# A two-layer decoder on one core: the last expert blocks in a branch, heads reordered, zeros by DMA, routing steps doubled

## The chip, the cores and the metric

The kernel runs on one core of one Trainium2 chip. A core has TensorE (PE, with its weight loads as PEld), VectorE (DVE), ScalarE (ACT), GpSimd (POOL) and SyncE (SP), each with a queue of its own, and 16 DMA engines that move what the queues issue. The metric is device microseconds (us) of one execution. Times from the profile come from one profiled execution.

## The reference

`x` has 4 images of 256 tokens with 256 features, `ctx_512` 4 x 256 x 64. Six blocks add to `x`, each after a layer norm: in layer 0 a latent attention (16 heads), an attention without weights of its own over the context, and a block that works on the 32 highest-scored tokens per image; in layer 1 these three:

```python
# head attention: for each token, its 16 heads attend to its 16 heads
q, k, v = (qkv[:, :, 0], qkv[:, :, 1], qkv[:, :, 2])           # each (b, n, 16, 16)
attn = jnp.einsum('bnhd,bngd->bnhg', q, k) / jnp.sqrt(jnp.float32(c))
attn = jax.nn.softmax(attn, axis=-1)
out = jnp.einsum('bnhg,bngd->bnhd', attn, v)
...
# cross attention: causal, 16 heads, keys and values from ctx_512
kv = latent_kv @ Wkv_expand.T
...
# experts: 28, the best 6 for each of the 1024 tokens
logits = x @ gate_weight.T
scores = jax.nn.softmax(logits, axis=-1)
topk_w, topk_idx = jax.lax.top_k(scores, TOP_K)
...
h = jax.nn.silu(x @ wg) * (x @ wu)
return (y + w_tok[:, None] * (h @ wd), None)
```

The inputs are drawn from a fixed seed. 1024 tokens times 6 choices are 6144 rows for the experts.

## The kernel before, in words

All of it is one program without loops on the chip: Python loops write out every instruction, and a planner (the tile framework) orders them for each engine. It goes by the order in which the program wrote them, and lets a later one go first where its inputs are ready earlier by its own estimate. Products that go through `_InOrder` (L72; the profile has them under L89 and L92) keep their written order. The written order of two pieces of work that run beside one another is made by `_side_by_side` (L54): each piece is a generator, one `yield` is one step, and the piece with the smallest share of its given number of steps done goes next.

Each of the later stages works in two halves of 512 tokens, images 0 and 1 and then 2 and 3.

*Heads and cross attention* (L534 to L569). `_head_attention` (L1203) gives two generators, `heads_a` and a second half. Per half it normalizes four row tiles (`ln_stats` with a rsqrt on POOL, L130; `h`, L146), transposes them (`h_tp`), and then takes four groups: `project` makes `pqkv` on PE and copies it on ACT, `weigh` multiplies q with k on POOL, eight heads at a time (L1270, 128x2048 elements), and sums on DVE (L1276); `combine` weights the values on DVE (L1295, L1302). At the end `o_tp` and `apo` (L1326) project out, and L1327 adds to `x`. `_cross_attention` (L1335) gives four generators: `context_kv(0)`, `context_kv(1)` and two halves. `context_kv` clears `vz` on POOL (L1368), and projects the context: `xpk` to keys, `xpv` to values, both through the two PSUM banks of tag "tp". A half waits until its pair of keys and values is there, and runs 16 steps of `scores` (`xsc`), `turned` (`x_tp`) and `values` (`xav`). L555 puts them side by side: the rest of `heads_a` and then the first cross half against `kv[0]`, the second half of the heads, and `kv[1]`. The second cross half follows alone (L567).

*Routing.* When an image leaves cross attention (`finish`, `xpo`, L1469), its generator goes on as `_route` (L585): layer norm into `R`, logits, the best six, the place of each row in its expert's list, and then twelve indirect DMAs from POOL (L676) that write the 128-row tiles of `R` into `lists` in HBM, one per choice and tile. `advance` (L1475) moves each waiting generator by one step; `half` calls it once per step of scores (L1530), and calls it in a loop when all scores are done (L1539).

*Experts.* `_blocks` (L686) makes from the counts of rows per expert the table of blocks: a block is 128 rows of one expert's list, and there is room for NBLK = 75, the most that any routing can need. A block beyond the last full list reads a list of blank rows, whose results land in rows that nobody reads. `_experts` (L731) runs the 75 blocks: SP loads `xb` four blocks ahead with an address from a register (L757), PE transposes it (`tpx`), multiplies with the gate and up weights of the block's expert (`pgu`, L781), DVE and ACT make `eh`, PE transposes (`tph`) and multiplies with the down weights (`py`, L804), ACT scales by the routing weight (`ys`), and POOL adds the rows into one of five accumulators in HBM by an indirect DMA (L809). Blocks below LATE = 41 take three accumulators in turn, the last 34 blocks the other two; the first three are read back and added to `x` (L843, L845) while the last blocks run, the other two at the end (L851 to L857).

At the start of the kernel SP fills `lists` and the accumulators from `blank`, a tile of zeros with a row number in column 256 (L513 to L524).

Of the kernel before, what the change touches and what calls it, by code (L numbers as in the profile page):

```python
# [19 lines left out]
P = 128  # L20
# [18 lines left out]
NACC = 3  # L39
NLATE, LATE = 2, NBLK - 34  # L40

# [25 lines left out]
def _in_turn(*gens):  # L67
    for gen in gens:
        yield from gen
# [34 lines left out]
def kernel(ctx: ExitStack, tc: tile.TileContext, w: dict, out: bass.AP):  # L104
# [311 lines left out]
    for _ in range(4):  # L416
# [13 lines left out]
    ms1 = mixed.enter_context(tc.tile_pool(name="mod_s", bufs=1, side="right"))  # L430
    mk = mixed.enter_context(tc.tile_pool(name="mod_k", bufs=2, side="right"))
    env = dict(
        psum=psum, sm=sm, cst=cst, ident=ident, identb=identb, maskb=maskb, tri=tri, ones=ones,
        ones_row=ones_row, layernorm=layernorm, ln_stats=ln_stats, ln_apply=ln_apply, rsqrt=rsqrt, transposed=transposed, ctxT=ctxT, neghalf=neghalf,
# [77 lines left out]
    acc = [dram.tile([B * S + P, C], F32, name=f"acc{n}") for n in range(NACC + NLATE)]  # L512
    blank = res.tile([P, ROW], F32, name="blank")  # L513
    nc.gpsimd.memset(blank, 0.0)
# [39 lines left out]
    kv = [next(cross) for _ in range(2)]  # L554
    _side_by_side((_in_turn(heads_a, next(cross)), 60), (_in_turn(kv[0], next(heads_of), kv[1]), 64))  # L555
    heads.close()
# [17 lines left out]
    for g in range(0, E, 7):  # L574
# [3 lines left out]
        )  # L578
    expert, list_row, e_all = _blocks(nc, tc, route)
    ps_stack.close()  # L580
    routing.close()
    _experts(nc, tc, x, out, dict(env, wgu=wgu, wdn=wdn, lists=lists, acc=acc, expert=expert, list_row=list_row, e_all=e_all))


# [101 lines left out]
def _blocks(nc, tc, env):  # L686
# [23 lines left out]
    nc.tensor.matmul(pe[:, 0], ones[:E], past, start=True, stop=True)  # L710
    nc.tensor.matmul(pe[:, 1], nbw, past, start=True, stop=True)
    e_all = rt1.tile([P, NBLK], F32, name="e_all")
    nc.vector.tensor_scalar(e_all, pe[:, 0], float(E - 1), None, ALU.min)
# [13 lines left out]
    nc.vector.tensor_scalar(list_row, row, float(TRASH // P), float(P), ALU.min, ALU.mult)  # L727
    return expert, list_row, e_all


def _experts(nc, tc, x, out, env):  # L731
# [4 lines left out]
    with tc.tile_pool(name="ek", bufs=2) as ek, tc.tile_pool(name="eb", bufs=AHEAD + 3) as eb, tc.tile_pool(  # L736
# [16 lines left out]
        def load(j):  # L753
            if j % ROWS == 0:
                at["row"] = values(list_row, mybir.EngineType.SP, TRASH, j, ROWS)
            xb = eb.tile([P, ROW], F32, tag="xb", name="xb")
            nc.sync.dma_start(xb, lists[bass.ds(at["row"][j % ROWS], P), :])  # L757
            return xb
# [31 lines left out]
        def down(j, hT, e, xb):  # L790
# [12 lines left out]
            for k in range(2):  # L803
# [5 lines left out]
            nc.gpsimd.indirect_dma_start(  # L809
                out=acc[j % NACC] if j < LATE else acc[NACC + (j - LATE) % NLATE],  # L810
                out_offset=bass.IndirectOffsetOnAxis(ap=xb[:, C : C + 1].bitcast(I32), axis=0),
# [13 lines left out]

        words = values(expert, mybir.EngineType.PE, (1 << 20) - 1, 0, NW)
        xbs = {j: load(j) for j in range(AHEAD)}
        xTs = {j: turned(xbs[j], 0, P, "x") for j in range(2)}
        before = None
        for j in range(NBLK):  # L830
            if j + AHEAD < NBLK:
                xbs[j + AHEAD] = load(j + AHEAD)
            h, e = gate_up(j, xTs.pop(j))
            if before is not None:
                down(*before)
            if j + 2 < NBLK:
                xTs[j + 2] = turned(xbs[j + 2], 0, P, "x")
            before = (j, turned(h, 0, MH, "h"), e, xbs.pop(j))
# [7 lines left out]
        down(*before)  # L846

# [355 lines left out]
def _head_attention(nc, tc, x, w, env):  # L1203
# [20 lines left out]
    def half(g):  # L1224
# [36 lines left out]
        def weigh(j):  # L1261
# [5 lines left out]
            for c in range(2):  # L1267
                hh = slice(8 * c, 8 * c + 8)
                pr = a2.tile([P, 8, H, D], F32, tag="qk", name="qk")
                nc.gpsimd.tensor_tensor(  # L1270
                    pr,
                    q3[:, hh].unsqueeze(2).to_broadcast([P, 8, H, D]),
                    k3.unsqueeze(1).to_broadcast([P, 8, H, D]),
                    ALU.mult,
                )
                nc.vector.tensor_reduce(s[:, hh], pr, AX.X, ALU.add)  # L1276
                yield
# [57 lines left out]
def _cross_attention(nc, tc, x, w, env):  # L1335
# [28 lines left out]
    def context_kv(bp):  # L1364
        tok = slice(bp * 512, (bp + 1) * 512)
        kz = c1.tile([P, 2, 2, 512], F32, name=f"kz{bp}")
        vz = vzs[bp]
        nc.gpsimd.memset(vz, 0.0)  # L1368
        for n in range(4):
# [150 lines left out]
    def half(bp):  # L1520
# [3 lines left out]
        for b in (2 * bp, 2 * bp + 1):  # L1524
            ss = c2.tile([P, 2, H], F32, tag="xss2", name="xss2")
            for n in range(8):
                g, e, sp = n // 4, n // 2 % 2, n % 2
                now = (f, b, g, e, sp, scores(f, b, g, e, sp, ss), ss)
                yield
                advance()  # L1530
                waiting.append(now)
                if len(waiting) > 2:
                    after(*waiting.pop(0))
                yield
        if bp == 1:
# [124 lines left out]
```

## Time and profile before

| | |
|---|---|
| time, median of 3 runs | 972.06 us (971.18 to 975.4) |
| the profiled execution | 971.14 us |
| its span, first to last instruction | 969.3 us |
| PE busy | 772.9 us, 80% |
| DVE busy | 546.7 us, 56% |
| POOL busy | 332.8 us, 34% |
| ACT busy | 306.5 us, 32% |
| mean granted clock of TensorE | 0.838 |

| stretch of the span | what runs |
|---|---|
| 0 to 440 us | layer 0, and from 305 us on the first half of the heads beside it |
| 440 to 620 | heads, first cross half, context keys and values |
| 620 to 706 | second cross half, routing of images 0 and 1 |
| 706 to 745 | routing of images 2 and 3, writes of the lists |
| 745 to 951 | 75 expert blocks |
| 951 to 969 | last sums, output |

A line of the profile names a source line (L781), an engine, and the tiles written and read (`pgu<-wgu_e,Tx`). The chain of work is followed back from the last instruction: at each step to what released it. Busy time of PE includes matmuls that wait in its pipeline; idle time of an engine costs something only where others wait for that engine.

### The profile page before, as it was taken

The numbers are of one execution on the slowest core, as the hardware profiler recorded it, in microseconds if no ns is written. First come the engines' busy times: TensorE is split into PE (matmuls) and PEld (weight loads), VectorE is DVE, ScalarE is ACT, GpSimd is POOL, SyncE is SP. The second block draws the span as 40 slices with busy tenths as digits, with TensorE's granted clock in tenths as the row PEclk, the third lists the DMA queues.
The fourth block names the chain that finished last, engine by engine and source line by source line (L and its number), as shares of the span: only waits on it lengthen the run. The fifth ranks groups of instructions, "written<-read, shape, count | busy, mean of one in ns | idle before, by whom it ended". The sixth has DMA issues, their size and how long they took to land.

```text
span 969.3 us, 12208 instructions
## 1 busy us (share of the span) xinstructions
PE 772.9 (80%) x3740; PEld 484.5 (50%) x3740; DVE 546.7 (56%) x1334; ACT 306.5 (32%) x997; POOL 332.8 (34%) x247
## 2 busy tenths in 40 slices
PE   5989999699898675637858699977940999988992
PEld 2555556355565332414524456555530777766771
DVE  3277556966543688894499685346630333344333
ACT  1145434441521211211202343345400344433440
POOL 2022122214210357212650300053154466655663
PEclk9899989789997697675766659788875999999997
DMA  9689999101315004101000001921067466686666
GB/s 304 190 269 325 325 326 349 57 1 52 122 45 217 3 0 173 44 0 30 1 0 1 1 0 65 353 74 44 31 183 214 68 113 113 110 193 123 112 105 155
DMA packets 85902, 118.49 MB, mean 122 GB/s; under 512 B 5485, under 2 KB 73903, under 8 KB 85328
## 3 DMA queue, kind: packets, MB, share of 16 engines
q1 hardware_dynamic: 71072, 99.22, 31.5%
q0 software_dynamic: 13104, 16.92, 11.1%
q10 hardware_dynamic: 1664, 1.57, 0.5%
q8 instruction: 33, 0.54, 0.2%
q14 instruction: 29, 0.24, 0.1%
HBM read 60.66 MB, written 57.03 MB: 121 GB/s over the span
## 4 chain that ended last, share of the span: by engine, by line
PE 49%; DVE 18%; SPq 10%; POOL 7%; DMA 7%; issue 4%; ACT 4%; another core or an unknown queue 0%; DVEq 0%; ACTq 0%; POOLq 0%
PE pgu L781 9%; SPq L519 8%; PE py L804 6%; POOL qk L1270 4%; PE xsc L89 4%; PE x_tp L92 3%; DMA part<-acc 2%; DVE s L1276 2%; SPq L522 2%; PE tph L763 2%; DVE pv L1295 2%; PE tpx L763 2%; POOL lists L676 1%; DVE O L1302 1%; PE pqkv L1254 1%
## 5 line engine op out<-in xcount | busy, mean ns | idle before, releaser
L809 POOL DMA_INDIRECT acc<-ys,xb x75 | 117.1, 1562 | 95.4 <-ACT Tx L766 75.5
L781 PE MATMUL pgu<-wgu_e,Tx 128*128 x300 | 106.4, 477 | 2.1 <-issue 2.1
L330 POOL TENSOR_TENSOR pr<-pr,rs 128x512 f32<-128x512 f32 x32 | 42.0, 1311 | 166.9 <-DVE rs L328 78.2
L1270 POOL TENSOR_TENSOR qk<-qkv 128x2048 f32<-128x2048 f32 x16 | 72.0, 4523 | 71.4 <-ACT qkv L1258 42.3
L804 PE MATMUL py<-wdn_e,Th 88*128 x300 | 78.0, 382 | 0.6 <-DVE Th L768 0.6
L320 ACT ACTIVATE pr<-sc,nb 128x256 f32<-128x256 f32 x128 | 59.0, 474 | 61.4 <-DVE nb L315 61.2
L676 POOL DMA_INDIRECT lists<-R,rows x48 | 46.7, 973 | 77.6 <-DVE rows L660 46.9
L804 PEld LDWEIGHTS py<-wdn_e,Th 88*128 88x128 f32 x300 | 57.1, 191 | 21.6 <-DVE Th L768 1.0
L1413 ACT ACTIVATE xpr<-xsc,cnm 128x256 f32<-128x256 f32 (+1 forms) x128 | 52.2, 422 | 40.2 <-DVE cnm L1408 28.6
L787 DVE TENSOR_TENSOR eh<-pgu,sg 128x176 f32<-128x176 f32 x75 | 25.6, 341 | 68.8 <-ACT sg L785 37.3
L781 PEld LDWEIGHTS pgu<-wgu_e,Tx 128*128 128x128 f32 x300 | 51.8, 192 | 21.1 <-issue 4.4
L1276 DVE TENSOR_REDUCE s<-qk 128x128 f32<-128x2048 f32 x16 | 36.5, 2279 | 35.0 <-POOL qk L1270 35.0
L793 DVE SCALAR_TENSOR_TENSOR wjunk<-cst,e_all,xb 128x28 f32<-128x28 f32 x75 | 18.5, 247 | 63.7 <-ACT ys L808 44.4
L808 ACT ACTIVATE ys<-py,wsel 128x256 f32<-128x256 f32 x75 | 35.6, 474 | 43.7 <-PE py L804 41.5
L89 PE MATMUL av<-pT,ckt 128*64 128x256 f32 x256 | 41.7, 423 | 9.4 <-DVE pT L346 9.2
L311 DVE TENSOR_REDUCE nm<-sc 128x4 f32<-128x1024 f32 x32 | 39.0, 1218 | 17.5 <-PE sc L89 17.4
L785 ACT ACTIVATE sg<-pgu 128x176 f32<-128x176 f32 x75 | 23.8, 318 | 78.8 <-PE pgu L781 74.2
L89 PE MATMUL xsc<-kz,xqT 32*128 32x256 f32 (+1 forms) x256 | 41.9, 424 | 7.2 <-ACT xpr L1413 4.6
L92 PE MATMUL x_tp<-cst,xpr 128*128 128x128 f32 x192 | 37.0, 336 | 12.0 <-DVE xpT L1429 5.8
L763 PE MATMUL tpx<-cst,xb 128*128 128x128 f32 x150 | 29.3, 279 | 20.3 <-DMA xb<-lists 20.3
L89 PE MATMUL sc<-ckv,qk 64*128 64x256 f32 x256 | 41.0, 422 | 1.5 <-ACT qk L298 0.7
L92 PE MATMUL tp<-cst,pr 128*128 128x128 f32 x256 | 38.0, 289 | 3.3 <-DVE pT L346 2.4
(318 smaller groups left out, 1577.9 us busy)
## 6 DMA issues: line engine op xcount, KB each, us to landing
lists<-blank SPq DMA_DIRECT2D x9, 3600.0 KB
xb<-lists SPq DMA_DIRECT2D x75, 144.0 KB
wgu_e<-in_e_gu_dram SPq DMA_DIRECT2D x4, 2464.0 KB
acc<-blank SPq DMA_DIRECT2D x5, 1152.0 KB
wdn_e<-in_e_dn_dram SPq DMA_DIRECT2D x4, 1232.0 KB
wq<-in_m_wq_dram SPq DMA_DIRECT2D x4, 1024.0 KB
mwo<-in_m_wo_dram SPq DMA_DIRECT2D x2, 2048.0 KB
part<-acc SPq DMA_DIRECT2D x16, 256.0 KB
```

The source lines that it names most:

```text
L89: self._next(self.engine.matmul(*args, **kw))
L92: self._next(self.engine.transpose(*args, **kw))
L320: nc.scalar.activation(pr[:, e, qt, :], sc[:, e, qt, :], AF.Exp, bias=nb[:, e, qt : qt + 1], accum_out=ss[:, e, qt : qt + 1],)
L519: nc.sync.dma_start(part, blank.unsqueeze(1).to_broadcast([P, 25, ROW]))
L676: put = nc.gpsimd.indirect_dma_start(out=lists, out_offset=bass.IndirectOffsetOnAxis(ap=rows[:, i, n : n + 1], axis=0), in_=R[:, i, :], in ...
L763: nc.tensor.transpose(tp[:m, k, :], src[:, c0 + k * m : c0 + (k + 1) * m], ident)
L781: nc.tensor.matmul(pg, xT[:, k, :], wgu[:, bass.ds(e * (4 * M) + k * 2 * M, 2 * M)], start=(k == 0), stop=(k == 1))
L804: nc.tensor.matmul(py, hT[:, k, :], wdn[:, bass.ds(e * (2 * C) + k * C, C)], start=(k == 0), stop=(k == 1))
L809: nc.gpsimd.indirect_dma_start(out=acc[j % NACC] if j < LATE else acc[NACC + (j - LATE) % NLATE], out_offset=bass.IndirectOffsetOnAxis(ap= ...
L1270: nc.gpsimd.tensor_tensor(pr, q3[:, hh].unsqueeze(2).to_broadcast([P, 8, H, D]), k3.unsqueeze(1).to_broadcast([P, 8, H, D]), ALU.mult,)
L1276: nc.vector.tensor_reduce(s[:, hh], pr, AX.X, ALU.add)
L1413: nc.scalar.activation(pr[:, j, cols], sc[:, j, cols], AF.Exp, bias=nm[:, i, j : j + 1], accum_out=ss[:, i, h : h + 1])
```

## The change

Five things change.

1. Blocks 64 to 74 stand in a branch (`tc.If`), ahead of blocks 0 to 63 in the program. `total`, the number of blocks that the routing needs, is one more product in `_blocks`; all engines load it and jump over the branch where it is at most 64. The loop body is the same, moved into `blocks(first, end, also)`. LATE becomes 30, so that the last 34 of the 64 blocks use the two late accumulators; blocks in the branch use the first three. The address registers are loaded for up to five blocks at a time, as before, from the start of each part.
2. The second half of the heads writes its first eight steps (norm, transposes, the first group's projection and first product), then come both pairs of context keys and values, then the rest of the heads. The numbers of the two sides are 60 and 60 instead of 60 and 64.
3. The products of q and k on POOL come as two instructions of four heads instead of one of eight. DVE's sum over them stays one instruction.
4. `vz` is cleared by two DMAs per pair from `blank` on SP's queue instead of a memset on POOL. `blank` is allocated earlier for that.
5. While the last image's scores run, `advance` is called twice per step.

```diff
-NLATE, LATE = 2, NBLK - 34
+USUAL = 64
+NLATE, LATE = 2, USUAL - 34
...
-    _side_by_side((_in_turn(heads_a, next(cross)), 60), (_in_turn(kv[0], next(heads_of), kv[1]), 64))
+    heads_b = next(heads_of)
+
+    def second():
+        for _ in range(8):
+            next(heads_b)
+            yield
+        yield from _in_turn(*kv, heads_b)
+
+    _side_by_side((_in_turn(heads_a, next(cross)), 60), (second(), 60))
...
+    pt = psum.tile([P, 8], F32, tag="tp", name="ptotal")
+    nc.tensor.matmul(pt[:1, 0:1], nb, ones[:E, 0:1], start=True, stop=True)
+    total = rt1.tile([1, 1], I32, name="total")
+    nc.vector.tensor_copy(total, pt[:1, 0:1])
...
-                out=acc[j % NACC] if j < LATE else acc[NACC + (j - LATE) % NLATE],
+                out=acc[j % NACC] if j < LATE or j >= USUAL else acc[NACC + (j - LATE) % NLATE],
...
         words = values(expert, mybir.EngineType.PE, (1 << 20) - 1, 0, NW)
-        xbs = {j: load(j) for j in range(AHEAD)}
-        xTs = {j: turned(xbs[j], 0, P, "x") for j in range(2)}
-        before = None
-        for j in range(NBLK):
...
+        xbs = {}
+
+        def blocks(first, end, also=None):
+            for j in range(first, first + AHEAD):
+                if j not in xbs:
+                    xbs[j] = load(j)
+            xTs = {j: turned(xbs[j], 0, P, "x") for j in range(first, first + 2)}
+            before = None
+            for j in range(first, end):
+                if j + AHEAD < end:
+                    xbs[j + AHEAD] = load(j + AHEAD)
+                h, e = gate_up(j, xTs.pop(j))
+                if before is not None:
+                    down(*before)
+                if j + 2 < end:
+                    xTs[j + 2] = turned(xbs[j + 2], 0, P, "x")
+                before = (j, turned(h, 0, MH, "h"), e, xbs.pop(j))
+                if also is not None:
+                    also(j)
+            down(*before)
...
+        more = nc.values_load(
+            env["total"], min_val=0, max_val=NBLK, skip_runtime_bounds_check_because="a sum of rounded counts, at most NBLK"
+        )
+        with tc.If(more > USUAL):
+            blocks(USUAL, NBLK)
+        blocks(0, USUAL, join_sums)
...
-                nc.gpsimd.tensor_tensor(
-                    pr,
-                    q3[:, hh].unsqueeze(2).to_broadcast([P, 8, H, D]),
-                    k3.unsqueeze(1).to_broadcast([P, 8, H, D]),
-                    ALU.mult,
-                )
+                for i in range(2):
+                    h0 = 8 * c + 4 * i
+                    nc.gpsimd.tensor_tensor(
+                        pr[:, 4 * i : 4 * i + 4],
+                        q3[:, h0 : h0 + 4].unsqueeze(2).to_broadcast([P, 4, H, D]),
+                        k3.unsqueeze(1).to_broadcast([P, 4, H, D]),
+                        ALU.mult,
+                    )
                 nc.vector.tensor_reduce(s[:, hh], pr, AX.X, ALU.add)
...
-        nc.gpsimd.memset(vz, 0.0)
+        for e in range(2):
+            nc.sync.dma_start(vz[:, :, e], env["blank"][:, :C].unsqueeze(1).to_broadcast([P, 4, C]))
...
                 if len(waiting) > 2:
                     after(*waiting.pop(0))
+                if b == B - 1:
+                    advance()
                 yield
```

More of the change, by code (lines that the diff above doesn't have):

```diff
@@ L431 @@
     mk = mixed.enter_context(tc.tile_pool(name="mod_k", bufs=2, side="right"))
+    blank = res.tile([P, ROW], F32, name="blank")
     env = dict(
-        psum=psum, sm=sm, cst=cst, ident=ident, identb=identb, maskb=maskb, tri=tri, ones=ones,
+        blank=blank, psum=psum, sm=sm, cst=cst, ident=ident, identb=identb, maskb=maskb, tri=tri, ones=ones,
         ones_row=ones_row, layernorm=layernorm, ln_stats=ln_stats, ln_apply=ln_apply, rsqrt=rsqrt, transposed=transposed, ctxT=ctxT, neghalf=neghalf,
@@ L512 @@
     acc = [dram.tile([B * S + P, C], F32, name=f"acc{n}") for n in range(NACC + NLATE)]
-    blank = res.tile([P, ROW], F32, name="blank")
     nc.gpsimd.memset(blank, 0.0)
@@ L578 @@
         )
-    expert, list_row, e_all = _blocks(nc, tc, route)
+    expert, list_row, e_all, total = _blocks(nc, tc, route)
     ps_stack.close()
     routing.close()
-    _experts(nc, tc, x, out, dict(env, wgu=wgu, wdn=wdn, lists=lists, acc=acc, expert=expert, list_row=list_row, e_all=e_all))
+    _experts(nc, tc, x, out, dict(env, wgu=wgu, wdn=wdn, lists=lists, acc=acc, expert=expert, list_row=list_row, e_all=e_all, total=total))
 def _route(nc, tc, x, b, env):
@@ L727, in _blocks @@
     nc.vector.tensor_scalar(list_row, row, float(TRASH // P), float(P), ALU.min, ALU.mult)
-    return expert, list_row, e_all
+    return expert, list_row, e_all, total
 def _experts(nc, tc, x, out, env):
@@ L753, in load @@
         def load(j):
-            if j % ROWS == 0:
-                at["row"] = values(list_row, mybir.EngineType.SP, TRASH, j, ROWS)
+            if j not in at:
+                n = min(ROWS, (USUAL if j < USUAL else NBLK) - j)
+                for i, r in enumerate(values(list_row, mybir.EngineType.SP, TRASH, j, n)):
+                    at[j + i] = r
             xb = eb.tile([P, ROW], F32, tag="xb", name="xb")
-            nc.sync.dma_start(xb, lists[bass.ds(at["row"][j % ROWS], P), :])
+            nc.sync.dma_start(xb, lists[bass.ds(at.pop(j), P), :])
             return xb
@@ L826, in _experts, with join_sums @@
         words = values(expert, mybir.EngineType.PE, (1 << 20) - 1, 0, NW)
-        xbs = {j: load(j) for j in range(AHEAD)}
-        xTs = {j: turned(xbs[j], 0, P, "x") for j in range(2)}
-        before = None
-        for j in range(NBLK):
[L831 to L838, printed above, removed]
+        xbs = {}
[17 more added lines that the diff above has]
+            down(*before)
+        def join_sums(j):
             if 0 <= j - LATE - 3 < len(adds):
@@ L845, in _experts @@
                 nc.vector.tensor_tensor(x[t], x[t], parts[n, t // 2][:, t % 2, :], ALU.add)
-        down(*before)
+        more = nc.values_load(
[4 more added lines that the diff above has]
+        blocks(0, USUAL, join_sums)
         oview = out.rearrange("b (t p) c -> (b t) p c", p=P)
```

## The prediction

> **What bounds the kernel now.** I read the table of stretches first: it shows where TensorE is full and where it waits.
>
> ```profile
> 440.00:460.00 20.00, 17.65 (x35) 9.94 (x36) 8.24 (x20) 3.86 (x10) 5.48 (x6) 0.50 0.13 36
> 480.00:500.00 20.00, 16.70 (x34) 8.53 (x32) 17.68 (x26) 1.70 (x4) 9.53 (x4) 0.64 0.00 0
> 500.00:520.00 20.00, 9.36 (x34) 4.68 (x34) 18.54 (x13) 0.94 (x2) 8.23 (x2) 0.66 0.00 0
> 705.00:747.00 42.00, 8.29 (x36) 6.59 (x34) 9.50 (x54) 0.54 (x2) 23.98 (x25) 0.59 0.69 209
> 765.00:855.00 90.00, 90.00 (x429) 68.23 (x427) 33.15 (x142) 37.21 (x106) 55.96 (x36) 1.00 0.68 112
> ```
>
> Columns: the stretch, its length, then busy us of PE, PE's weight loads, DVE, ACT and POOL, granted clock, DMA share, GB/s. Three places matter. From 765 on, the expert blocks keep PE busy 90.00 us of 90 at clock 1.00: PE sets the pace. From 705 to 747 PE has 8.29 us of work: this is the tail of the routing. From 440 to 520 DVE, POOL and PE take turns.
>
> The chain of work, from the blocks' stage, shows the pace of one block:
>
> ```profile
> 764.56 1.26 PE pgu L781 x4
> 765.82 0.86 PE py L804 x4
> 767.12 1.25 PE pgu L781 x4
> ...
> 850.38 1.31 PE pgu L781 x4
> ```
>
> From 764.56 to 850.38 there are 34 blocks: 85.82 / 34 = 2.524 us each, all PE.
>
> POOL's timeline shows the tail (start, us, line, idle time before and its releaser):
>
> ```profile
> 706.64 1.05 POOL L676 DMA_INDIRECT lists<-R,rows  x1 [16.81 <-DVE rows L660]
> 714.32 0.96 POOL L676 DMA_INDIRECT lists<-R,rows  x1 [0.30 <-issue]
> 715.31 0.74 POOL L130 TENSOR_TENSOR ln_rs<-ln_ve,neghalf 128x2 f32<-128x2 f32 x1
> 726.15 0.96 POOL L676 DMA_INDIRECT lists<-R,rows  x1 [3.81 <-issue]
> 740.08 0.96 POOL L676 DMA_INDIRECT lists<-R,rows  x1 [0.30 <-issue]
> ```
>
> Image 2's twelve list writes start at 706.64, 1.27 us apart. Image 3's rsqrt, whose input was ready at 709.3 (ln_ve, DVE), stands behind seven of them until 715.31. Image 3's writes then run 726.15 to 741.04 and land at 744.9; only then does SP load the first block.
>
> The timelines of POOL and DVE at the start of the cross attention:
>
> ```profile
> 444.95 1.80 POOL L1368 MEMSET vz<- 128x2048 f32 x1
> 467.79 17.99 POOL L1270 TENSOR_TENSOR qk<-qkv 128x2048 f32<-128x2048 f32 x4 [17.84 <-ACT qkv L1258]
> 447.47 2.95 DVE L146 TENSOR_SCALAR h<-x_in,ln_mv,aln_rs 128x256 f32<-128x256 f32 x4 [0.70 <-POOL aln_rs L130]
> 472.31 2.29 DVE L1276 TENSOR_REDUCE s<-qk 128x128 f32<-128x2048 f32 x1 [21.89 <-POOL qk L1270]
> 499.02 9.68 DVE L146 TENSOR_SCALAR h<-x_in,ln_mv,cln_rs 128x256 f32<-128x256 f32 x4 [0.90 <-POOL cln_rs L130]
> ```
>
> The second half of the heads has its normalized rows at 450.4, but its first product starts at 467.79, because the context keys and values (xpk, xpv) hold PE and the two "tp" banks from 448.12 to 458.7. DVE idles 21.89 us for it.
>
> **The change part by part.** The sum is against the profiled execution, 971.14 us (span 969.3 and 1.8 around it); the median of the runs is 972.06, 0.9 above.
>
> *Blocks in a branch.* How many blocks carry tokens follows from the data: the reference's routing of its inputs gives the 28 experts 117 to 302 tokens, and their counts rounded up to 128 make 62 blocks. 62 is under 64, so blocks 64 to 74 are skipped: 11 x 2.524 = 27.8 us off, bounds 27.4 to 28.5 (single periods of 2.49 to 2.59). LATE moves from 41 to 30, so the sums of the first three accumulators stay as far from the end as now, and the stall around them (block 44 came 5.83 us after block 43, block 48 5.21 after 47) stays too. What is added: one product and one copy for `total` (the like of cnt, 0.14 us on DVE at 724.5), a load of it on all five engines, a compare and a jump. They are covered: the tables are ready at 728.4 and DVE then waits 19.03 us, PE 20.33 us, for the first block. Without that cover, if an engine can't pass the branch before the lists have landed, the row from landing to first product prices it: 744.91 to 750.79, 5.9 us. Bounds 0 to +6; I take +2, nearer to the covered end. A jump also has to find its code. The profile has the instruction queue:
>
> ```profile
> q8 instruction: 33, 0.54, 0.2%
> ```
>
> 33 packets with 0.2% of 16 engines' span: 0.002 x 16 x 969.3 / 33 = 0.94 us each, once on the jump, inside the cover. [...]
>
> The experts' words are now loaded on PE ahead of the branch. Before, the chain has 1.33 us of "issue" at 749.46 between block 0's turned rows and its first product, which I read as that load: -1.3 (0 to -2).
>
> *Routing steps doubled while the last image runs.* Image 2's route now advances twice per step of image 3. By the code its list rows came with the first advance behind image 3's eight steps, and come now with the sixth step: three steps sooner. A step's scores start 4.5 us apart here (eight of them from 662.9 to 694.1), so rows come near 705.7 - 13.5 = 692, and the twelve writes take 12 x 1.27 = 15.2, to some 708. Image 3's rsqrt finds POOL free at 709.3 instead of 715.31: -6.0. Its writes then end at 735 and the landing moves alike. The same work enters PE's queue earlier, between image 3's scores, and may hold them: 0.5 us back. -5.5; bounds -9 (if POOL's 3.81 idle goes as well) to +4 (the 3.10 us that DVE waits for PE's xpo before 685.30, once more and a little). On SP the wdn loads move with the end of cross attention.
>
> *Heads ahead of keys and values, zeros by DMA.* The two memsets leave POOL; with them go ln_ve's stretch (1.19 instead of 0.16 us) and one of h's (1.83 instead of 0.41), 2.4 us between 445.6 and 450.4. The heads' transposes no longer wait for xpv at 458.7. From them to the first product took 467.79 - 458.63 = 9.2; from 448 to 450.4 that gives 457.2 to 459.6, 8 to 10.6 sooner: -9. Keys and values of the second pair move from 606.52 to 619 on the chain (pieces of 3.30, 2.00, 1.06) into the holes of 455 to 520, where PE is busy 9.36 of 20 us: -6. Against it, the second half of the heads (38 of its 46 steps) now follows both, and thread weights 60:60 place its last x sums nearer to the last scores of the first pair. Before, 29 us lay between them (600.24) and the second pair's first scores (629.1), covered by three steps of scores; with less cover, +2. The zeros are four DMAs of 512 KB on SP, behind wxo at 446.16, with nothing behind them on SP until 600.15. The same kind of write, 3600 KB from `blank`, took about 11 us, so 1.6 each by size, and wxk's landing took 3.02: they are there before the copies into vz. Sum -13. Bounds -25 (PE idles 20.5 us between 440 and 520, and 4.5 of the stretched rows below) to +8 (xpk and xpv, 7.16 + 3.41, put in front of cross attention's own start at 510 with only 2 to 3 us hidden).
>
> *Products by four heads.* A 128x2048 product takes 4487 ns, a 128x512 one at L1032 1270 ns: 2.09 ns per element and 0.2 fixed, so two halves cost 0.2 more, 16 x 0.2 = 3.2 on POOL. About half of POOL's 72 us stands on the chain (3.8% of 969.3 = 37): +1.6. DVE instructions that run into a product stretch to its end: outside the rows of cross attention these are six between 346 and 480, longer than their kind by 0.8 to 2.2 us each, 8.2 in all; halved, -4, of which about half on the path, -2; and L1035 at 385.35, which waits for two whole products (chain: 376.51 to 385.35), may slip between: -1. In all -1.5, bounds +4 (all extra fixed costs on the path) to -8.
> The rows of cross attention themselves hold two stretched h (9.68 us for four). [...]
>
> Sum: 971.1 - 27.8 + 2 - 1.3 - 5.5 - 13 - 1.5 = 924.0; as a median 925.
>
> **Rivals.**
> *The order gives nothing.* The heads' late end uncovers the second pair's start. For it: DVE is busy 16 to 18.5 of 20 us from 480 to 580, so an earlier start may only meet it earlier. Against: its 21.89 idle. Time: 925 + 13 = 938, to 944 if the routing's gain goes too.
> *The order gives more.* Cross attention's first pair starts with the heads (516 could become 495): 925 - 12 = 913.
> *The branch is taken,* the change not doing what it says. It would need 65 blocks. No 27.8, and a second fill (5.9) and drain (946.86 to 949.1 without a next block, and some): 925 + 27.8 + 9 = 962.
> *Slower: the clock.* The blocks run at granted 1.00, the heads at 0.50 to 0.71. If the denser work ahead made the throttle grant the blocks 0.66, as from 500 to 520, 64 x 2.524 = 161.5 us become 244.7: 925 + 83 = 1008. It decides from a clock of 0.76 down: 47 us of gain and 4.9 more are 52, and 161.5 / (161.5 + 52) = 0.76. Against: every full stretch of blocks shows 1.00, and the low values stand where PE pauses.
>
> **How the numbers follow.** Forecast (914 to 937) 0.58; order gives nothing 0.22; more 0.11; branch taken 0.03; clock 0.03; the rest, mishaps that eat the gain, 0.03. The range leaves out the lower half of "more", and the last three: 906 to 945. A measurement of this kernel tells 0.5%, 4.9 us, from no change: faster 0.95, same 0.02, slower 0.03.
>
> **What would show it.** 64 groups of four pgu at 2.52 us; no xb load beyond 64; the first list write of image 2 before 700 and image 3's rsqrt with no write between its input and it; landing to first product under 5.9 us; the first product of the heads' second half some 9 us after their rows; xpk of the second pair before 520. Wrong it would be with 75 blocks, a gap of over 6 us at the branch, or a hole of PE over 15 us between heads and second pair.

## The result, and the profile after

The changed kernel takes 935.83 us (median of 933.57, 934.35, 937.30 and 953.64) beside 972.47 for the kernel before in the same session: ratio 0.9611, 95% interval 0.9574 to 0.9648. The profiled execution took 933.57 us, span 931.3 us. The forecast was 925, between 906 and 945. Some runs of these programs are about 20 us longer at a lower granted clock (below, seven of the ten of x2_old_order, the traced one among them); the ratios leave those out, which is why a ratio below can lie under that of the medians.

The span became 38.0 us shorter. The table follows both traces from stage to stage (us; the starts and ends are rows of the timelines, rounded to 0.1 us before they are subtracted).

| stage | before | after | measured | predicted |
|---|---|---|---|---|
| start to first scores of cross attention's second half | 629.1 | 618.8 | -10.3 | -14.5 |
| those to the last x sum | 78.7 | 76.8 | -1.9 | +0.5 |
| last x sum to end of the last list write | 33.2 | 27.1 | -6.1 | -6.0 |
| last list write to first expert product | 9.8 | 15.2 | +5.4 | +0.7 |
| first to last block's product | 196.0 | 169.2 | -26.8 | -27.8 |
| last block's product to the end | 22.5 | 24.2 | +1.7 | 0 |

The table of stretches of the changed kernel (columns as before):

```profile
440.00:460.00 20.00, 18.71 (x48) 9.91 (x48) 5.30 (x19) 5.17 (x15) 5.61 (x6) 0.68 0.46 142
480.00:500.00 20.00, 19.32 (x43) 11.26 (x42) 6.23 (x14) 2.74 (x7) 3.84 (x3) 0.57 0.00 0
500.00:520.00 20.00, 14.75 (x48) 7.96 (x47) 16.38 (x20) 5.36 (x25) 6.35 (x3) 0.60 0.00 1
695.00:735.00 40.00, 6.50 (x31) 5.37 (x30) 8.74 (x50) 0.25 (x1) 12.96 (x14) 0.55 0.66 182
```

From 480 to 500 the roles have changed: PE has 19.32 us of 20 (16.70 before) and POOL 3.84 (9.53). From 695 to 735, the routing's tail, PE has 6.50 us in 40: this hole has not gone, and it holds the 5.4 us that came back.

The chain of work in the blocks:

```profile
785.46 1.23 PE pgu L797 x4
...
808.13 1.29 PE pgu L797 x4
```

Nine blocks lie between: 22.67 / 9 = 2.52 us each, as before. There are 64 of them.

POOL's timeline in the tail, then the start of the heads' second half on POOL and DVE:

```profile
666.20 0.72 POOL L131 TENSOR_TENSOR ln_rs<-ln_ve,neghalf 128x2 f32<-128x2 f32 x1
680.66 1.05 POOL L685 DMA_INDIRECT lists<-R,rows  x1 [13.74 <-DVE rows L669]
694.67 0.96 POOL L685 DMA_INDIRECT lists<-R,rows  x1 [0.30 <-issue]
697.13 0.72 POOL L131 TENSOR_TENSOR ln_rs<-ln_ve,neghalf 128x2 f32<-128x2 f32 x1 [1.51 <-DVE ln_ve L142]
707.77 1.04 POOL L685 DMA_INDIRECT lists<-R,rows  x1 [9.92 <-issue]
721.78 0.96 POOL L685 DMA_INDIRECT lists<-R,rows  x1 [0.30 <-issue]
```

```profile
456.30 9.23 POOL L1304 TENSOR_TENSOR qk<-qkv 128x1024 f32<-128x1024 f32 x4 [8.69 <-ACT qkv L1290]
460.96 2.29 DVE L1310 TENSOR_REDUCE s<-qk 128x128 f32<-128x2048 f32 x1 [12.58 <-POOL qk L1304]
490.99 1.38 DVE L147 TENSOR_SCALAR h<-x_in,ln_mv,cln_rs 128x256 f32<-128x256 f32 x4 [1.12 <-POOL cln_rs L131]
```

Image 2's list writes end at 695.63, and image 3's rsqrt at 697.13 waits for its own input (DVE ln_ve) and for no write. The heads' first product is at 456.30 (467.79 before). The four h before cross attention take 1.38 us; before they took 9.68, beside POOL's products.

What came back is on SP. Its waits from 695 to 740 (us in total, times, longest), and the timelines of SP and ACT:

```profile
SPq L876 <- SPq L876: 23.2, 2, 23.0
```

```profile
733.17 5.42 SPq L773 DMA_DIRECT2D xb<-lists  x7
```

```profile
736.19 1.28 ACT L782 ACT_TABLE_LOAD   x1 [32.93 <-PE tpx L779]
737.49 0.65 ACT L782 COPY Tx<-tpx 128x256 f32<-128x256 f32 x2
740.70 1.28 ACT L801 ACT_TABLE_LOAD   x1 [2.56 <-issue]
```

SP reaches the branch (L876) at 708.18, and its next work is at 731.97. The lists land at 727.9 (DVE's wait for them ends there), but the first load leaves SP at 733.17, 5.2 us later; before, it left 0.2 us after. ACT loads its table again ahead of the first turned row (+1.28, on the path) and again for the first block's gate.

SP's own rows of the trace (start, operation, ns), above of the changed kernel and below of x8_pool_loads, where the branch's loads go by another queue:

```
708.18 COMPARE_BRANCH 50
708.38 EVENT_SEMAPHORE 17
731.40 EVENT_SEMAPHORE 17
...
731.97 TENSOR_LOAD 552

732.68 COMPARE_BRANCH 50
734.12 TENSOR_LOAD 567
```

Past the branch SP goes through eight semaphores of its own DMAs. The first of them (100 in the trace) holds it until 731.40. It is the one that the last of the four wdn loads counts up (issued on SP's queue from 695.21 on, this one at 699.08): the last packet of these loads is done at 730.9, and the last count comes at 731.39. Of the prediction's signs of being right one is missing here: from the landing of the lists to the first product it is 10.0 us (727.9 to 737.91), not under 5.9; a gap of over 6 us at the branch is what the prediction named as a sign of being wrong.

### The profile page after: what moved, and what is told of

The parts are those of the page before. It is cut to its first block, busy times and chain, and to the rows that moved or that the text cites. A ratio compares the mean times of both kernels' runs of the same rounds, so it can differ in the third digit from the quotient of the medians.

```text
span 931.3 us, 11708 instructions
## 1 busy us (share of the span) xinstructions
PE 737.9 (79%) x3610; PEld 461.0 (49%) x3610; DVE 522.0 (56%) x1291; ACT 296.4 (32%) x965; POOL 311.6 (33%) x250
## 5 line engine op out<-in xcount | busy, mean ns | idle before, releaser
L825 POOL DMA_INDIRECT acc<-ys,xb x64 | 99.7, 1558 | 91.4 <-ACT Tx L782 56.9
L1304 POOL TENSOR_TENSOR qk<-qkv 128x1024 f32<-128x1024 f32 x32 | 74.2, 2349 | 72.3 <-ACT qkv L1290 72.3
L797 PE MATMUL pgu<-wgu_e,Tx 128*128 x256 | 91.7, 481 | 0.8 <-ACT Tx L782 0.8
L820 PE MATMUL py<-wdn_e,Th 88*128 x256 | 67.0, 383 | 0.6 <-DVE Th L784 0.6
L1310 DVE TENSOR_REDUCE s<-qk 128x128 f32<-128x2048 f32 x16 | 36.6, 2285 | 41.8 <-POOL qk L1304 41.8
L820 PEld LDWEIGHTS py<-wdn_e,Th 88*128 88x128 f32 x256 | 48.7, 191 | 18.8 <-DVE Th L784 1.4
L803 DVE TENSOR_TENSOR eh<-pgu,sg 128x176 f32<-128x176 f32 x64 | 21.8, 341 | 58.4 <-ACT sg L801 58.4
L797 PEld LDWEIGHTS pgu<-wgu_e,Tx 128*128 128x128 f32 x256 | 44.5, 194 | 17.0 <-issue 1.3
L779 PE MATMUL tpx<-cst,xb 128*128 128x128 f32 x128 | 25.4, 282 | 27.1 <-DMA xb<-lists 27.1
L824 ACT ACTIVATE ys<-py,wsel 128x256 f32<-128x256 f32 x64 | 30.4, 474 | 38.0 <-PE py L820 37.4
L801 ACT ACTIVATE sg<-pgu 128x176 f32<-128x176 f32 x64 | 20.3, 318 | 65.0 <-PE pgu L797 63.9
```

The lines of the kernel that those rows point to most:

```text
L779: nc.tensor.transpose(tp[:m, k, :], src[:, c0 + k * m : c0 + (k + 1) * m], ident)
L797: nc.tensor.matmul(pg, xT[:, k, :], wgu[:, bass.ds(e * (4 * M) + k * 2 * M, 2 * M)], start=(k == 0), stop=(k == 1))
L820: nc.tensor.matmul(py, hT[:, k, :], wdn[:, bass.ds(e * (2 * C) + k * C, C)], start=(k == 0), stop=(k == 1))
L825: nc.gpsimd.indirect_dma_start(out=acc[j % NACC] if j < LATE or j >= USUAL else acc[NACC + (j - LATE) % NLATE], out_offset=bass.IndirectOf ...
L1304: nc.gpsimd.tensor_tensor(pr[:, 4 * i : 4 * i + 4], q3[:, h0 : h0 + 4].unsqueeze(2).to_broadcast([P, 4, H, D]), k3.unsqueeze(1).to_broadca ...
```

## The experiments

All times are device us; each group shared one chip. "Write to load" and "to product" are from the end of the last list write to the first xb load and the first expert product, read from each trace (the times are rounded to 0.1 us before they are subtracted).

| kernel | median | ratio, 95% interval | second half to last sum | sum to last write | write to load | to product |
|---|---|---|---|---|---|---|
| before (first trace) | 972.06 | | 78.7 | 33.2 | 4.1 | 9.8 |
| after (first trace) | 935.83 | 0.9611, 0.9574 to 0.9648 | 76.8 | 27.1 | 10.5 | 15.2 |
| x1_no_branch | 951.91 | 0.9787, 0.9709 to 0.9866 | 100.4 | 27.1 | 5.5 | 12.6 |
| x7_ahead | 960.14 | 0.9852, 0.9745 to 0.9958 | 102.7 | 27.3 | 5.6 | 12.1 |
| x8_pool_loads | 956.47 | 0.9831, 0.9750 to 0.9912 | 101.6 | 27.1 | 6.8 | 11.6 |
| x6_taken | 990.05 | 1.0168, 1.0085 to 1.0250 | 102.7 | 27.3 | 5.5 | 10.3 |
| x2_old_order | 969.83 | 0.9814, 0.9782 to 0.9846 | 88.9 | 27.3 | 10.8 | 15.6 |
| x3_eight | 933.57 | 0.9629, 0.9572 to 0.9685 | 76.6 | 27.1 | 10.4 | 15.1 |
| x4_memset | 936.00 | 0.9622, 0.9584 to 0.9660 | 75.4 | 27.3 | 10.7 | 15.5 |
| x5_single | 928.60 | 0.9556, 0.9520 to 0.9592 | 68.6 | 33.2 | 5.5 | 10.2 |
| x14_after_again | 960.97 | 0.9837, 0.9798 to 0.9877 | 99.8 | 26.8 | 10.5 | 15.1 |
| x11_wide_wdn | 955.09 | 0.9787, 0.9746 to 0.9828 | 102.8 | 27.4 | 5.0 | 9.7 |
| x12_single_wide_ahead | 942.95 | 0.9652, 0.9612 to 0.9693 | 83.9 | 33.3 | 1.7 | 11.9 |
| x10_branch_alone | 951.60 | 0.9762, 0.9706 to 0.9818 | 81.3 | 33.2 | 6.4 | 11.1 |

### First group: what the branch costs (kernel before here: 979.74)

*x1_no_branch*: no branch; blocks 64 to 74 are left out altogether.

```
-        more = nc.values_load(env["total"], ...)
-        with tc.If(more > USUAL):
-            blocks(USUAL, NBLK)
         blocks(0, USUAL, join_sums)
```

> Blocks 64 to 74 and the branch are left out of the program; `total` is still computed and nobody reads it. For these inputs the 64 blocks are enough. Theory (the branch costs 5 to 6 us between the landing of the lists and the steady blocks): landing to first product 5.9 us again or 1 to 2 less, time 5 to 7 us under the changed kernel, 929 to 931. Rival (the branch costs nothing, the lists only land later beside the wdn loads): landing to first product stays near 10 us, time within 2 us of 935.8.

*x7_ahead*: the loads of blocks 0 to 3 ahead of the branch, into buffers of their own.

```
-        xbs = {}
+        xbs = {j: load(j, "xb0", AHEAD) for j in range(AHEAD)}
```

> The loads of blocks 0 to 3 stand ahead of the branch, in four buffers of their own; all else as in the changed kernel. Theory (SP, behind the branch, waits for DMAs issued earlier, the wdn loads, before it issues the first loads): first load within 1 us of the landing, first product 3.5 to 5 us sooner, time 931 to 932. ACT still loads its table again behind the branch. Rival (the jump itself, PE's 7.1 us in the branch instruction, is what the blocks wait for): PE still gets to its first product 10 us behind the landing, time 935 to 936.

*x8_pool_loads*: inside the branch the loads go by POOL's queue.

```
+            queue, engine = (nc.sync, SP) if j < USUAL else (nc.gpsimd, Pool)
-            nc.sync.dma_start(xb, ...)
+            queue.dma_start(xb, ...)
```

> Only inside the branch, which is skipped, the loads go by POOL's queue instead of SP's. Theory (a skipped branch makes the engine whose DMAs it holds settle their counts, for which that engine waits for its earlier DMAs): SP passes at once, first load within 1.5 us of the landing, time 931 to 933; POOL settles its counts when the lists have landed, and has 18 us until its first scatter. Rival (SP waits for something other than the counts of its own DMAs): the first load stays 5.2 us behind the landing, time 935 to 936.

*x6_taken*: `more > 0`, so that all 75 blocks are computed.

> The condition is made true always, so all 75 blocks run, 64 to 74 first. Prediction's price: 27.8 for the blocks and 9 for a second fill and drain, 935.8 + 36.8 = 972.6. Rival by what the skipped branch showed (the count settling and ACT's table load come at the end of the branch either way): 4 to 6 us more, 977 to 979.

The total times of this group miss what was expected of the three that skip the blocks, and not for the branch: 24 to 26 us more than in the first trace of after lie in the second half of cross attention, which none of the edits touches. (PE and POOL run the same instructions in the same order there as in after.) The third group takes this up. The stage behind the lists can be read all the same. Without the branch the first load comes 5.5 us after the last write, and with it 10.5; 5.6 if SP has issued the first loads before the branch, and 6.8 if the branch has no loads of SP's. In x7_ahead the first product comes 3.1 us sooner than in after (12.1 against 15.2), where 3.5 to 5 were expected. Among SP's waits x8_pool_loads has none at the branch (L877); the lists are waited for:

```profile
SPq L774 <- DMA lists<-R,rows: 6.1, 1, 6.1
```

So it is not the branch as such that held SP. In after, where the skipped branch holds loads of SP's queue, SP waits 23.0 us there, until the last wdn load's count; in x8_pool_loads, where it holds none, SP does not wait there. Without the branch the first product still comes 12.6 us after the last write, because the experts' words are then loaded on PE in the path again (2.03 us) instead of ahead of it; against x8_pool_loads (11.6) the branch costs nothing there.

The chain of x6_taken, where the eleven blocks run before block 0:

```profile
781.01 1.19 PE pgu L797 x4
...
790.95 3.69 DMA acc<-ys,xb
794.83 2.14 DMA xb<-lists
797.77 2.46 PE pgu L797 x4
```

The second fill and drain put 11.75 us between the last of these blocks' products and block 0's, 9.2 more than a period. From first product to end it takes 231.9 us, x8_pool_loads 195.8: 36.1 more, where the prediction's rival had 27.8 + 9 = 36.8. ACT loads its table again here too, behind the eleven blocks (790.87, 1.28 us) and off this chain.

### Second group: the parts of the order and the routing (kernel before: 971.91)

*x2_old_order*: heads, and context keys and values, in the old order.

```
-    _side_by_side((_in_turn(heads_a, next(cross)), 60), (second(), 60))
+    _side_by_side((_in_turn(heads_a, next(cross)), 60), (_in_turn(kv[0], next(heads_of), kv[1]), 64))
```

> Only the written order of heads and context keys and values is put back (weights 60 and 64, keys and values of the first pair first); the other four parts stay. Theory (the order brings 10 to 12 us at the first cross half's start, of which some is lost again where the heads end late): first scores of the first half near 516 instead of 505, time 943 to 948. Rival (the order gives nothing, the gain there came from the zeros and the products): time within 3 us of 935.8.

*x3_eight*: one product for eight heads, as before.

```
-                for i in range(2):
...
+                nc.gpsimd.tensor_tensor(pr, q3[:, hh]..., k3..., ALU.mult)
```

> Only the products of the heads go back to eight heads at a time. Prediction's term: 1.5 us dearer, 937.3. Rival (halves only add their fixed cost, 16 x 0.2 us, and DVE's instructions pass one per half, so nothing is won): 1 to 3 us cheaper, 933 to 935.

*x4_memset*: zeros by POOL.

```
-        for e in range(2):
-            nc.sync.dma_start(vz[:, :, e], ...)
+        nc.gpsimd.memset(vz, 0.0)
```

> Only the zeros go back to memsets on POOL. Prediction's term: 2.4 us dearer, 938.2. Rival (the memsets now stand behind the first group's products and hide, since keys and values come later): within 1 us of 935.8.

*x5_single*: one routing step per step of the last image.

```
-                if b == B - 1:
-                    advance()
```

> Only the second call of advance for the last image is taken out. Prediction's term 5.5 us, the traces 6.0 from the last sum into x to the last list write: 941 to 942, with image 3's rsqrt again behind list writes of image 2. Rival (the lists wait for the wdn loads on the DMA engines, so an earlier issue does not land earlier): within 2 us of 935.8.

The order carries the gain of this part. The changed kernel itself did not run on this chip, so x3_eight stands in for it: x2_old_order against x3_eight, 0.9814 - 0.9629 = 1.85%, 18 us. By the ends of the two intervals it is between 1.0 and 2.7%, 9 to 27 us. Products by four and zeros by DMA are worth nothing that can be seen: 0.9629 and 0.9622 beside 0.9611, each well inside the others' intervals. These reach 4 to 6 us to either side, so the 1.5 and 2.4 us that were predicted could not have shown in them. DVE's rows tell the first apart, h in x3_eight and then in x2_old_order:

```profile
492.22 1.38 DVE L147 TENSOR_SCALAR h<-x_in,ln_mv,cln_rs 128x256 f32<-128x256 f32 x4 [1.12 <-POOL cln_rs L131]
```

```profile
496.89 7.41 DVE L147 TENSOR_SCALAR h<-x_in,ln_mv,cln_rs 128x256 f32<-128x256 f32 x4 [0.90 <-POOL cln_rs L131]
```

With the old order and products by four these four take 7.41 us (9.68 by eight): halving gives 2.3. With the new order no product lies beside them and they take 1.38, by eight too. The order had taken away what the halves were to mend.

Undoing the doubled routing steps makes the kernel faster, the best of all that ran: 928.6 against 933.6 and 936.0 on the same chip, 5 to 7 us. The doubling does what it says behind the last sum (33.2 to 27.1), and costs more ahead of it: the last sum comes at 695.6 in after and at 687.9 in x5_single. Together the last write ends 1.6 us later with the doubling (722.7 against 721.1). Part of the 7.7 is one hole on PE, shown here for after and then x5_single:

```profile
667.52 0.66 PE L613 MATMUL g_tp<-cst,R 128*128 128x128 f32 x2 [8.45 <-DVE R L147]
```

```profile
666.88 0.66 PE L613 MATMUL g_tp<-cst,R 128*128 128x128 f32 x2 [4.83 <-DVE R L147]
```

Both wait for image 2's rsqrt, which stands behind image 1's list writes on POOL (666.20 above). In after PE's hole is 3.6 us longer. The other 4 us I put down to the work itself, now done between the last image's steps, where the granted clock is 0.53 (from 660 to 680; 0.66 in x5_single); no run takes them apart.

The rest of the loss is the branch. In x5_single SP's settling took as long as the lists, and its first load followed at once:

```profile
SPq L876 <- SPq L876: 17.9, 2, 17.7
```

```profile
726.60 5.42 SPq L773 DMA_DIRECT2D xb<-lists  x7
```

The settling ended at 724.68, the lists' last packet at 724.5, wdn's at 724.1. The wdn loads start when cross attention ends and take 36.1, 35.4 and 36.2 us from the last sum in before, after and x5_single, whatever the routing does. In before they ended at 743.9 and the lists landed at 744.9: two bounds of the same height. The doubling lowered one of them. The traces of after and x5_single differ by 4.1 us in all: 1.6 at the last write and 5.0 from there to the first product, less 2.5 that x5_single loses again from the first product to the end (195.9 against 193.4). This loss lies between blocks 32 and 40 (28.0 us against 24.9), where the first sums are read back; x7_ahead and x8_pool_loads are as long there (27.4 and 26.4), and no run tells why.

### Third group: the wdn loads, and the chip (kernel before: 977.15)

While wdn loads, 11 packets of SP's queue are under way at a time (11.1 on average from 697 to 714 in after), and 16 while wgu loads (16.5 from 609.5 to 618). Each wdn load ends there in 11 counts of its semaphore (the last one's from 729.61 to 731.39), an xb load in 16 (734.99 to 735.32). wdn has 88 partitions.

*x14_after_again*: the changed kernel, unaltered.

> The changed kernel once more, unaltered, as the base of the three others on their chip: 933 to 938, its first xb load 10.5 us after the last list write, as in its first trace. If the long second half of cross attention that the four kernels of the first group showed (100 to 103 us from its first scores to the last x sum, instead of 77) belongs to the chip and not to those kernels, this one may show it too and be near 955.

*x11_wide_wdn*: each wdn load cut in two.

```
-        nc.sync.dma_start(wdn[:, ...], w["e_dn"][g : g + 7]...)
+        for p0, p1 in ((0, 80), (80, MH)):
+            nc.sync.dma_start(wdn[p0:p1, ...], w["e_dn"][g : g + 7, p0:p1]...)
```

> Changed kernel, each wdn load cut into partitions 0 to 79 and 80 to 87. In the trace of after, 11 packets of SP's queue are under way at a time while wdn loads (16 while the wgu loads go), and they go on to 731.0, 35.4 us after the last x sum. Theory (at the branch SP first lets its own unfinished loads land, the wdn loads among them): with 5 and 1 of 88 partitions on an engine instead of 8 they end some 35.4 x 6/8 = 26.6 us after the last sum, near 722, ahead of the lists; the first xb load then comes 4 to 6 us after the last list write instead of 10.5, and the time falls by 4 to 6 us against after on this chip. Rival 1 (the branch itself takes 5 us of SP, whatever is under way): first load still 10 to 11 us after the last write, time as after. Rival 2 (the wdn loads are held by the list writes on the same engines, not by the 11): SP's queue ends as late as before, no change.

*x12_single_wide_ahead*: x5_single's edit, this one, and x7_ahead's with the turned rows of blocks 0 and 1 ahead of the branch as well.

> Changed kernel with three edits: the last image's single routing steps, the wdn loads cut in two, and the loads of blocks 0 to 3 with the turned rows of blocks 0 and 1 ahead of the branch. Theory: x5's first product came 10.2 us after the last list write, of which 1.28 is ACT's table load behind the branch and the rest the lists' landing, the load and the turning; with the rows turned ahead of the branch the table load leaves the path, 8 to 9.5 us: 924 to 928 where x5 had 928.6, 8 to 12 below after on this chip. Rival (the wait for wdn moves from the branch to the first down product, or PE pays its 7 us branch between the turned rows and the first product): 929 to 936.

*x10_branch_alone*: the kernel before with the branch and nothing else of the change.

> The kernel before, with only the branch edited in (blocks 64 to 74, the total, the words ahead of the branch, LATE). Theory: there the wdn loads leave SP's queue near 744 and the lists land at 744.9, so that settling them costs SP little: first xb load 4 to 6 us after the last list write, 64 blocks at 2.52, ACT's table load (+1.3) against the words (-1.3): 26 to 28.5 us under before. Rival (the branch costs 5 us wherever it stands): 20 to 24 us under before.

The stretch from the last sum to the first load, in x14_after_again and then x11_wide_wdn:

```profile
718.00:756.00 38.00, 6.51 (x33) 5.32 (x31) 8.74 (x50) 0.25 (x1) 12.32 (x13) 0.56 0.67 181
```

```profile
718.00:748.00 30.00, 6.81 (x32) 5.56 (x30) 8.74 (x50) 0.25 (x1) 12.35 (x13) 0.54 0.95 227
```

The DMA share goes from 0.67 (11 / 16 = 0.69) to 0.95. The wdn loads end 29.3 us after the last sum instead of 35.1 (26.6 expected), ahead of the lists; the first load comes 5.0 us after the last write instead of 10.5, and the first product 9.7 instead of 15.1. The median falls by 5.9 us. Rival 1, a fixed price of the branch, and rival 2, wdn held by the list writes, are both out. The two ratios' intervals overlap slightly (0.9798 to 0.9877 against 0.9746 to 0.9828); the verdict on this stage rests on the traces' 5.4 us. From the first product to the end the trace of x11_wide_wdn is 2.2 us longer again (195.1 against 192.9), so how much of the 5.4 the time keeps is less sure.

x10_branch_alone does not decide by its time. Its median is 25.6 us under before, just outside what was expected (26 to 28.5); its ratio, 0.9762, is 23.3 us, inside the rival's 20 to 24, and its interval (18 to 29 us) holds both. The trace does decide: the wdn loads end at 759.1 and the lists at 758.9, SP is held by the last wdn load's semaphore until 759.53, and the first load follows at 761.00, 2.1 us behind the lists, where before it followed 0.7 us behind their last packet (744.43). So the branch cost SP some 1.4 us here and not 5.

x12_single_wide_ahead is 18 us faster than the changed kernel on its chip, so the single routing steps win here too; 12 of these are beside x11_wide_wdn. But its turned rows ahead of the branch were a mistake. PE's timeline:

```profile
740.80 1.18 PE L780 MATMUL tpx<-cst,xb 128*128 128x128 f32 x4 [17.95 <-DMA xb<-lists]
748.68 2.10 PE L798 MATMUL pgu<-wgu_e,Tx 128*128 x3 [6.70 <-PEq L878]
```

PE loads the words (1.85 us) and then takes 3.86 us for the jump, both now between the turned rows and the first product: 11.9 us from write to product, not the 8 to 9.5 expected. This was the rival named for it. The same edits without the rows ahead were not run.

x14_after_again settles that the long second half is not the work of the first group's edits: the unaltered kernel has it here, with 961 us. With doubled routing steps all six traces on this chip and the first group's have some 100 us there, and the four others have 75 to 89, so I put it down to the chip; the chip of the first trace of after is not on record. The stretch from 618 to 634 in after (first) and here (second), and DVE's timeline here:

```profile
618.00:634.00 16.00, 15.87 (x150) 10.96 (x149) 11.72 (x27) 10.11 (x44) 9.61 (x10) 1.00 1.04 409
```

```profile
618.00:634.00 16.00, 9.54 (x65) 5.00 (x63) 4.29 (x9) 2.35 (x10) 9.69 (x11) 0.79 1.03 408
```

```profile
625.62 0.56 DVE L1464 COPY xpT<-x_tp 128x384 f32<-128x384 f32 x1 [4.21 <-remote]
...
632.73 0.69 DVE L1442 TENSOR_REDUCE cnm<-xsc 128x2 f32<-128x512 f32 x1 [5.81 <-remote]
...
711.04 1.02 DVE L1464 COPY xpT<-x_tp 128x384 f32<-128x384 f32 x2 [8.05 <-remote]
```

The profile writes "remote" where it finds no instruction or DMA that ended just before the release. DVE sits before rows whose matmuls ended long before: the last one's x_tp ended at 706.1, and the semaphore by which PE releases it rises at 711.01, as the trace has it. So what is late is PE's release (or its matmuls, whose ends the profile models), and not DVE. Waits with this releaser sum to 29.1 us on DVE here; in after, x3_eight, x4_memset and x5_single there is none. They have one thing in common: each ends while POOL is in a burst of list writes or at most 2.4 us behind one (615.6 to 630.7, 659.3 to 674.2, 693.8 to 708.8 here). With doubled steps image 2's burst falls into the last image's scores; in x12_single_wide_ahead it starts at 702.4, 1.1 us before the last sum. That fits the second halves here, 99.8 and 102.8 with doubled steps, 83.9 and 81.3 without. What delays PE's releases in a burst, and why it shows in every trace on these two chips and elsewhere only in that of before (7.0 us, 1.7 of them on DVE and 5.3 on ACT), stays open.

## Why the prediction was right, and where its steps were not

The time fell inside the range, and 36.6 of 47 us came. The blocks, the largest term, were right; three others (order, routing, branch) missed by 5 to 12 us each and partly cancelled (the branch's 5 us are also part of what the routing steps cost). That the sum still fell inside the range is in part luck.

- **Blocks: right.** -26.8 of -27.8; 2.52 us each, at a granted clock of 1.00 or near it (0.98 from 750 to 840). The clock rival did not come, nor did the taken branch, whose price x6_taken confirms.
- **The branch's cover: the step "They are covered" failed.** It looked at DVE's and PE's waits of 19 and 20 us. These two did pass in the cover (PE's jump took 7.10 us and cost nothing); SP did not. The text had said that the wdn loads move with the end of cross attention, and gave this no price. The bound had the right size, 5.9 us, but the value was taken at the covered end; +5.4 was measured for +0.7. x11_wide_wdn removes it. "Inside the cover" was right for the jump of PE, though its own price, 0.94 us, was not: it took 7.10.
- **Experts' words: right, and paid back.** The 2.03 us load left the path (x1_no_branch shows it there again); ACT's table load, 1.28 us, came in.
- **Routing steps doubled: "0.5 us back" failed.** Behind the last sum it gave -6.1 for the -6.0 worked out, and image 3's rsqrt stood behind no write. Ahead of it the same work cost 7.7 us, fifteen times what was set down, and the SP wait came on top. A gain of 5.5 was a loss of 5 to 7.
- **Order of the heads: right in its mechanism, too small.** First product 11.5 us earlier (9), the second pair's keys and values at 465 to 490 instead of 606 to 619, heads' last sum 7 us later (607.2) and the second pair's scores still 10.3 us sooner. Undone, it costs 18 us (-13 predicted). By x5_single's trace some 10 of these lie in the second half (68.6 against 78.7), which the sum did not have. Before has 7.0 us of the "remote" waits there and x5_single none; whether they account for it was not tested. On the third group's chip the second half is no shorter with the new order (83.9 in x12_single_wide_ahead, 81.3 in x10_branch_alone), so where these 10 us come from stays open. And the four h at 499 were counted at nothing: they fell by 8.3 us, because the order took the products away from beside them.
- **Products by four: -1.5 was nothing** that can be measured, and for the stretched h the rows show why. The sum counted nothing for these four, and x2_old_order shows 2.3 us less beside halves (7.41 for 9.68). The 4.5 us of them in the order's bound of -25 is shown by no run: 2.3 came beside halves, and 8.3 where no product lay beside them.

## What to carry to other kernels

When a tail is shortened, list everything else that starts at the same event and ends near the same time: here the weight loads ended 1 us before the lists, and 5 us of the gain fell to them. Price a branch on every engine by what that engine still has under way, above all on the one that issues DMAs: here SP waited 23.0 us at it with the wdn loads under way, and PE's jump took 7.10. Price work moved from an idle tail into a busy stage in that stage: here it cost 7.7 us, where 0.5 had been set down.

## What the runs showed of the hardware

- **The load of 88 partitions kept 11 packets under way at a time,** and ended in 11 counts. Cut into 80 and 8, the same bytes took 29.3 us instead of 35.1, at DMA shares of 0.95 and 0.67. That 11 of the 16 engines carry it is an estimate from these counts and from the share (11 / 16 = 0.69 beside 0.67).
- **The jump costs PE 7.06 to 7.74 us** where it skips the blocks and the wdn loads run (3.86 in x12_single_wide_ahead, where they have ended), 45 to 72 ns on the other engines, and 0.09 us on PE in x6_taken, which falls through. In each of these jumps, and not in x6_taken, one 16 KB packet of the instruction queue moves. In after it starts 4.60 us into the jump and takes 1.05, and PE goes on 1.45 behind it; in x12_single_wide_ahead these are 1.01, 1.43 and 1.43. So in after, with the wdn loads under way, most of the jump (4.60 of 7.10 us) passes before the packet starts, and the prediction had priced the packet alone, at 0.94.
- **SP waits for its unfinished loads behind the skipped branch** in after (23.0 us, to the last wdn load's count at 731.39), where the branch holds loads of SP's queue. There is no such wait in x8_pool_loads, where it holds none, and none in x6_taken, which runs the blocks and has its first load 5.5 us after the last write. **ACT loads its table again behind the branch,** skipped or not (1.28 us; at 736.19 in after, at 790.87 in x6_taken, absent in x1_no_branch).
- **One kernel, 936 us when it first ran and 961 in the third group.** The second half of cross attention has 23 us of the difference (99.8 against 76.8), and only the longer one has waits around POOL's list writes there (29.1 us on DVE, 11.8 on ACT). That the waits make the difference fits the traces, and no run shows it alone.
